# Seeding four RNN steps at once, and transposing before the tanh

## The chip, the cores and the metric

The kernel runs on one core of a Trainium2 chip. The metric is the time of one execution on the device in microseconds. The engines are named as in the profile: PE is the matrix engine (TensorE), PEld its weight loads, DVE is VectorE, ACT is ScalarE, POOL is GpSimd, SP is the engine that issues most DMAs.

## The reference, cut to what matters

The kernel computes two layers, each an attention branch and a feed-forward branch, on x of 8 sequences (batch B), 512 steps and 256 features in float32. The change lies in the last branch: a plain recurrent network over the 512 steps, followed by a mixture of 16 experts with two chosen per token.

```python
xW = jnp.einsum('ntd,dh->nth', x, Wx) + b

def step(h_prev, xw_t):
    h_next = jnp.tanh(xw_t + h_prev @ Wh)
    return (h_next, h_next)
_, hs = jax.lax.scan(step, h0, jnp.swapaxes(xW, 0, 1))
...
return x + _mlp(x, shared_wg, shared_wu, shared_wd) + expert_weighted
```

In the second part of the quotation x stands for the states hs. Each step needs the state of the step before, so the 512 steps run one after another: 8 rows of 256 features times a matrix of 256 x 256, plus the input's share xW, then tanh.

## The kernel before, in words

Earlier stages (attention of layer 0, an LSTM of 512 steps, routed heads, attention of layer 1) are not touched. The last stage is `rnn_moe`; it begins at 3272 us of the span.

**The recurrence.** The state is kept transposed, with the 256 features as 2 x 128 partitions, in `ring`: 16 steps (a chunk, `XB`) x 2 halves k x 32 columns, of which the first 8 hold the batch. `rnn_step` does one step t. Its 8 recurrent matmuls (L1375) take the state of the step before as the stationary operand (128 rows x 8 columns, for each half k) and 64 columns of `Wh` as the moving operand, for j = 0..3. Matmul j writes 8 rows at partitions 32j of the accumulator `pg` (128 x 64, one of two that alternate); so the four j lie in four column groups of PE. A float32 matmul is two passes on PE, so 8 matmuls are 16 PE records, in four passes of the four groups. The input's share of a step, `xw`, is brought into `pg` before that by four "seed" matmuls (L1359): the stationary operand is 8 columns of the identity matrix that pick the 8 rows of step t out of a chunk of 128 rows (b, t). The seeds of step t+1 are issued right behind the recurrent matmuls of step t. Then ACT takes the tanh of the whole `pg` (128 x 64) into `h` (L1379), and DVE transposes `h` in blocks of 32 x 32 into the ring's slot (L1380).

**What else shares the loop.** Each step ends with `consume()`, which issues the DVE and ACT work left over from the step before (`M.later`), and `advance(...)`, which issues one piece of PE work: the projection of a later chunk's input (`rnn_project`, L1349), a piece of a finished chunk (`Experts.chunk`: router L1428, turning the states L1439, shared expert L1450 to L1455, its second matmul L1468, residual L1472), or a piece of an expert tile (`Experts.tiles`: gate matmuls L1597, transposes of the next tile L1587, down matmul L1613). The order on PE, ACT and DVE is exactly the order of these calls (`manual_schedule`); each engine works through its list in order. So on PE a step is: recurrent matmuls, seeds, the piece of other work; on ACT: tanh, then later work; on DVE: transpose, then later work. A chunk's pieces fall on steps t%16 = 2, 3, 4, 7 and 8; tiles and projections take the others, where there are any. A tile takes three steps: a first gate step (half of the gate matmuls, first transpose), a second gate step (the other half, second transpose) and a down step. The transposes of a tile share a PSUM tile and are copied out one by one:

```python
nc.tensor.transpose(pt[:, k, :], X[m][:, k * P : (k + 1) * P], K.ident)
later(lambda: nc.scalar.copy(xT[:, k, :], pt[:, k, :]))
```

These are L1587 and L1588. The gate's later work is a sigmoid on ACT (L1606) and a product on DVE (L1607). The LSTM stage (L677 to L696, 457 to 1710 us) has the same layout of its state, but transposes the sums on DVE first and lets ACT work on the transposed block.

**Waits.** An instruction waits for its semaphores; where it has more than one, the others are waited for by an instruction of the sequencer ahead of it (EVENT_SEMAPHORE in the profile), in the order in which the program lists them.

**POOL.** It copies a finished chunk of the ring into `hT` (L1421), gathers x for projections and residuals (L1336), and issues the scatters and gathers of rows (L1558, L1650); some of these are held back until `M.pace`, which is the transpose of the current step.

Of the kernel before, what the change touches and what calls it, by code (L numbers as in the profile page):

```python
# [9 lines left out]
F32 = mybir.dt.float32  # L10
I32 = mybir.dt.int32
U32 = mybir.dt.uint32
AF = mybir.ActivationFunctionType
# [5 lines left out]
P = 128  # L19
B = 8  # L20
S = 512
# [1306 lines left out]
XB = 16  # L1328
# [3 lines left out]
def chunk_x(K, M, n, tag):  # L1332

    xc = M.hp.tile([P, 2, P], F32, name=tag, tag=tag)
    for k in range(2):
        K.nc.gpsimd.tensor_copy(xc[:, k].rearrange("p (b t) -> p b t", b=B), K.xT[:, k, :, n * XB : (n + 1) * XB])  # L1336
    return xc
# [14 lines left out]
            yield 1  # L1352


def rnn_seed(K, M, t):

    pick = K.ident.rearrange("p (b t) -> p t b", b=B)
    for j in range(4):
        K.nc.tensor.matmul(  # L1359
            M.pg[t % 2][32 * j : 32 * j + B], pick[:, t % XB, :], M.xw[:, t // XB, 64 * j : 64 * j + 64], start=True, stop=False  # L1360
        )


def rnn_step(K, M, t):


    nc, mm = K.nc, K.nc.tensor.matmul
    at = t % XB
    if at == 0:
        M.last, M.ring = M.ring, M.rg.tile([P, XB, 2, 32], F32, name="ring", tag="ring")  # L1370
    pg = M.pg[t % 2]
    for k in range(2):
        hp = K.h0T[:, k, :] if t == 0 else (M.ring[:, at - 1, k, 0:B] if at else M.last[:, XB - 1, k, 0:B])
        for j in range(4):
            mm(pg[32 * j : 32 * j + B], hp, M.wh[:, k, 64 * j : 64 * j + 64], start=False, stop=(k == 1))  # L1375
    if t + 1 < S:
        rnn_seed(K, M, t + 1)
    h = M.hp.tile([P, 64], F32, name="h", tag="h")
    nc.scalar.activation(h, pg, AF.Tanh)  # L1379
    M.pace = nc.vector.transpose(M.ring[:, at].rearrange("p k b -> p (k b)"), h)  # L1380


class Experts:
# [30 lines left out]
    def chunk(self, c, ring):  # L1414

        K, M, NE = self.K, self.M, self.NE
        nc, mm, later = K.nc, K.nc.tensor.matmul, M.later
        t0 = (self.first + c) * XB
        hT = M.hp.tile([P, 2, B, XB], F32, name="hT", tag="hT")
        for k in range(2):  # L1420
            nc.gpsimd.tensor_copy(hT[:, k], ring[:, :, k, 0:B].rearrange("p t b -> p b t"))  # L1421
        xc = chunk_x(K, M, t0 // XB, "xc")
        hk = [hT[:, k].rearrange("p b t -> p (b t)") for k in range(2)]
        yield 0
        yield 0
        pr = M.pd.tile([P, NE], F32, name="pr", tag="pd")
        for k in range(2):
            mm(pr, hk[k], M.wr[:, k, :], start=(k == 0), stop=(k == 1))  # L1428
        rl = M.sp.tile([P, NE], F32, name="rl", tag="rl")

        def logits():
            nc.vector.tensor_tensor(rl, pr, M.rb, ALU.add)
            nc.scalar.activation(rl, rl, AF.Sigmoid)

        later(logits)
        yield 1
        pt = M.pd.tile([P, 2, P], F32, name="pt", tag="pd")
        for k in range(2):
            nc.tensor.transpose(pt[:, k, :], hk[k], K.ident)  # L1439
        hr = M.ap.tile([P, D], F32, name="hr", tag="hr", bufs=16)  # L1440
        self.hr.append(hr)

        def turned():
            nc.scalar.copy(hr, pt.rearrange("p k t -> p (k t)"))
            nc.vector.max(out=self.top[:, c, :], in_=rl)
            nc.vector.max_index(out=self.topi[:, c, :], in_max=self.top[:, c, :], in_values=rl)

        later(turned)
        pw = [M.pgu.tile([P, P], F32, name="pw", tag="gu")]
        mm(pw[0], M.wg[:, 0, :], hk[0], start=True, stop=False)  # L1450
        yield 1
        mm(pw[0], M.wg[:, 1, :], hk[1], start=False, stop=True)
        pw.append(M.pgu.tile([P, P], F32, name="pw", tag="gu"))
        for k in range(2):
            mm(pw[1], M.wu[:, k, :], hk[k], start=(k == 0), stop=(k == 1))  # L1455
        a = M.sp.tile([P, P], F32, name="a", tag="a")

        def act():
            nc.scalar.activation(a, pw[0], AF.Sigmoid)
            nc.vector.tensor_tensor(a, pw[0], a, ALU.mult)  # L1460
            nc.vector.tensor_tensor(a, pw[1], a, ALU.mult)

        later(act)
        yield 1
        yield 0
        yield 0
        pd = M.pd.tile([P, D], F32, name="pd", tag="pd")
        mm(pd, a, M.wd, start=True, stop=False)  # L1468
        yield 1
        pj = pd.rearrange("p (j k r) -> p k j r", j=4, k=2)  # L1470
        for k in range(2):
            mm(pj[:, k], xc[:, k], K.ident, start=False, stop=(k == 1))  # L1472
        acc = M.ap.tile([P, D], F32, name="acc", tag="acc", bufs=27)
        self.acc.append(acc)
        later(
            lambda: nc.vector.tensor_tensor(
                acc.rearrange("p (j k r) -> p j k r", j=4, k=2),
                pd.rearrange("p (j k r) -> p j k r", j=4, k=2),
                hr.rearrange("p (k j r) -> p j k r", j=4, k=2),
                ALU.add,  # L1480
            )
        )
        yield 1
# [182 lines left out]
def rnn_moe(K, out):  # L1666


    nc, inp = K.nc, K.inp
    with ExitStack() as es:  # L1670
        wp = K.pool(es, "m_w")
        M = Scope()
# [34 lines left out]
        M.sp = K.pool(es, "m_s", 4)  # L1707
        M.wp = K.pool(es, "m_e", 7)
        M.ap = K.pool(es, "m_a", 2)
        M.rg = K.pool(es, "m_rg", 3)  # L1710
        M.hp = K.pool(es, "m_h", 2)
        M.psx = K.pool(es, "m_px", 1, PSUM)
        psg = K.pool(es, "m_pg", 1, PSUM)
        M.pg = [psg.tile([P, 64], F32, name=f"pg{i}") for i in range(2)]
        for t in M.pg:
            nc.vector.memset(t, 0.0)
        M.pxt = K.pool(es, "m_xt", 1, PSUM)
        M.pgu = K.pool(es, "m_gu", 2, PSUM)
        M.pd = K.pool(es, "m_pd", 2, PSUM)
        M.ring = None  # L1720
        xc = chunk_x(K, M, 0, "xp")
        px = M.psx.tile([P, D], F32, name="px", tag="px")
        for k in range(2):
# [1 line left out]
        nc.vector.tensor_tensor(M.xw[:, 0, :], px, M.rbias, ALU.add)  # L1725
        due = []
        M.later = due.append
        rnn_seed(K, M, 0)
        E = mybir.EngineType

        def consume():
# [32 lines left out]
        nb, at = -1, 0  # L1764
        with K.tc.manual_schedule(engines={E.PE, E.Activation, E.DVE}):
            for t in range(S):
                if t % XB == 0:
                    if t == XB * sum(BLOCKS[: nb + 1]):
                        nb += 1
                        block, at = Experts(K, M, nb), 0  # L1770
# [187 lines left out]
```

## Time and profile before

| | |
|---|---|
| median of 14 runs | 4100.07 us (4095.39 to 4108.0) |
| the profiled execution, its own time | 4097.13 us |
| its span | 4095.3 us |
| mean granted PE clock | 0.968 |
| busy share PE / PEld / DVE / ACT / POOL | 87% / 56% / 58% / 36% / 15% |
| the loop of 512 steps | 3286 to 3908 us, preceded by 8 us in which step 0 waits for ACT |
| granted PE clock in the loop | 0.94 |
| after the loop | 187 us for the last tiles and the output |

A line of the groups gives line, engine, operation, what is written and read, the shapes and the count; then the busy time in us and the mean ns of one; then how long the engine was idle before them and what ended most of that. In the order in time each line has start and duration in us, engine, line, operation and count, and in brackets the idle time before it and its releaser. Kernel lines in the profile of before are those of the listing above.

### The profile page before, as it was taken

The page shows a single profiled execution, that of the slowest core. Times are in us where ns is not written, and L with a number is a line of the kernel's source. Part 1 is how long each engine was busy: PE and PEld are TensorE (multiplying, and loading weights), DVE is VectorE, ACT ScalarE, POOL GpSimd, SP SyncE. Part 2 cuts the span into 40 slices and gives each one's busy share as a digit, 9 for nine tenths or more (in the row PEclk, how much of TensorE's full clock was granted, in tenths as well). Part 3 has the DMA queues.
Part 4 walks back from the last instruction along what each step waited for, and adds up shares of the span by engine and source line. Part 5 has one row for each costly group of instructions (what it writes and reads, how often), then busy time and mean ns, then how long its engine had stood idle before and what let it go on. Part 6 is the DMA issues. An engine that isn't in the chain of part 4 may idle for free.

```text
span 4095.3 us, 150218 instructions
## 1 busy us (share of the span) xinstructions
PE 3551.9 (87%) x64484; PEld 2275.7 (56%) x64484; DVE 2395.6 (58%) x8916; ACT 1463.1 (36%) x5391; POOL 606.2 (15%) x1250
## 2 busy tenths in 40 slices
PE   8899888888888888699988998999899887999885
PEld 5533455555555555456645555555555555767564
DVE  4488666666666666466657667656766533333332
ACT  3111233333333333245534435444444322333242
POOL 1010000000000000111012222222212221030412
PEclk9899999999999999899989999999999998999897
DMA  3122000000000000200000000000000022443476
GB/s 105 42 67 73 18 20 15 21 15 20 5 4 4 4 4 4 76 24 24 1 2 2 1 1 1 1 1 1 1 1 1 13 96 68 118 149 105 129 245 204
DMA packets 104844, 173.11 MB, mean 42 GB/s; under 512 B 12576, under 2 KB 71872, under 8 KB 103792
## 3 DMA queue, kind: packets, MB, share of 16 engines
q1 hardware_dynamic: 79792, 114.23, 9.1%
q0 software_dynamic: 12064, 34.34, 2.6%
q10 hardware_dynamic: 12320, 14.94, 1.1%
q8 instruction: 505, 8.27, 0.9%
q14 instruction: 163, 1.34, 0.1%
HBM read 124.53 MB, written 40.10 MB: 40 GB/s over the span
## 4 chain that ended last, share of the span: by engine, by line
PE 42%; DVE 8%; ACT 3%; DMA 2%; issue 2%; ACTq 0%; SPq 0%; POOL 0%; DVEq 0%; POOLq 0%
PE pg L1375 5%; PE pe L1202 4%; PE pp L1166 4%; DVE sm L1218 3%; PE pt L1241 3%; PE pg L1597 3%; PE px L1276 3%; PE po L1257 3%; DMA x<-xs 2%; PE pe L893 2%; PE pp L869 1%; PE pv L1186 1%; PE py L1613 1%; PE pt L913 1%; PE pg L1359 1%
## 5 line engine op out<-in xcount | busy, mean ns | idle before, releaser
L677 PE MATMUL pgi<-wh,ring 128*8 128x128 f32 x8176 | 319.3, 273 | 214.9 <-DVE ring L696 212.2
L1222 ACT ACTIVATE sm<-sm,nm 128x388 f32<-128x388 f32 (+3 forms) x512 | 282.9, 553 | 346.9 <-DVE nm L1218 346.8
L684 ACT ACTIVATE X<-G 128x32 f32<-128x32 f32 x512 | 117.1, 229 | 679.9 <-DVE G L683 679.9
L1380 DVE STREAM_TRANSPOSE ring<-h 128x64 f32<-128x64 f32 x512 | 125.6, 245 | 396.4 <-ACT h L1379 382.1
L677 PEld LDWEIGHTS pgi<-wh,ring 128*8 128x8 f32 x8176 | 177.1, 89 | 279.2 <-DVE ring L696 277.7
L1241 PE MATMUL pt<-ident,sm 128*128 128x128 f32 x1280 | 214.7, 284 | 104.6 <-ACT eT L1243 55.4
L683 DVE STREAM_TRANSPOSE G<-pgi 128x128 f32<-128x128 f32 x512 | 161.8, 316 | 244.8 <-PE pgi L677 244.8
L1379 ACT ACTIVATE h<-pg 128x64 f32<-128x64 f32 x512 | 114.7, 224 | 456.4 <-PE pg L1375 419.6
L1241 PEld LDWEIGHTS pt<-ident,sm 128*128 128x128 f32 x1280 | 144.2, 142 | 224.4 <-DVE eT L1243 86.9
L1375 PE MATMUL pg<-wh,ring 128*8 128x64 f32 x8176 | 219.9, 228 | 55.3 <-DVE ring L1380 51.0
L1166 PE MATMUL pp<-hn,wqkv 128*128 128x512 f32 x512 | 244.4, 604 | 5.0 <-DVE hn L1151 5.0
L1232 POOL COPY pme<-sm 128x4 f32<-128x4 f32 x512 | 119.6, 234 | 818.9 <-DVE sm L1231 814.6
L1375 PEld LDWEIGHTS pg<-wh,ring 128*8 128x8 f32 x8176 | 122.0, 91 | 163.7 <-DVE ring L1380 132.3
L677 PE MATMUL pgg<-wh,ring 128*8 128x64 f32 x8176 | 208.6, 219 | 1.3 <-issue 1.3
L677 PE MATMUL pgo<-wh,ring 128*8 128x64 f32 x8176 | 208.8, 219 | 0.1
L657 PE MATMUL pgi<-xw,ident 128*8 128x128 f32 x4096 | 207.7, 273 | 0.5 <-DVE xw L647 0.5
L1218 DVE CUSTOM_DVE_ANT_0 sm<-pe,mask 128x260 f32<-128x260 f32 (+2 forms) x384 | 141.7, 425 | 107.6 <-PE pe L1202 103.8
L696 DVE SCALAR_TENSOR_TENSOR ring<-to,th 128x16 f32<-128x16 f32 x512 | 89.6, 175 | 174.7 <-ACT th L695 174.7
L1243 ACT COPY eT<-pt 128x128 f32<-128x128 f32 (+3 forms) x256 | 108.4, 423 | 212.8 <-PE pt L1241 212.7
L1231 DVE TENSOR_SCALAR sm<-sm,rc 128x388 f32<-128x388 f32 (+3 forms) x512 | 177.3, 389 | 9.1
L1597 PE MATMUL pg<-xT,w 128*128 128x128 f32 x992 | 172.5, 300 | 10.6 <-DVE a L1460 8.9
L1202 PE MATMUL pe<-kt,qt 32*128 32x132 f32 (+3 forms) x2048 | 177.8, 461 | 0.0
(503 smaller groups left out, 7887.8 us busy)
## 6 DMA issues: line engine op xcount, KB each, us to landing
w<-in_experts_dram SPq DMA_DIRECT2D x124, 384.0 KB
cb<-order POOLq DMA_DIRECT2D x32, 512.0 KB, 4.1
x<-xs SPq DMA_DIRECT2D x124, 128.0 KB
ys<-y SPq DMA_DIRECT2D x124, 128.0 KB
xs<-zero ACTq DMA_DIRECT2D x2, 4736.0 KB
w<-in_ada_w_dram SPq DMA_DIRECT2D x16, 512.0 KB
w<-in_moh_w_dram SPq DMA_DIRECT2D x32, 192.0 KB
out_dram<-acc SPq DMA_DIRECT2D x32, 128.0 KB
```

What stands on the lines that cost most here:

```text
L657: mm(dst[32 * j : 32 * j + B], pick[:, t % XB, :], xw[:, j * 256 + lo : j * 256 + hi], start=True, stop=False)
L677: mm(dst[32 * j : 32 * j + B], hp, wh[:, k, j * 256 + lo : j * 256 + hi], start=False, stop=(k == 1))
L683: nc.vector.transpose(G[:, 0:2].rearrange("p g k b -> p (g k b)"), pgi[t % 2].rearrange("p g n -> p (g n)"))
L1166: mm(pp, T.wqkv[:, k, 0 : 2048].rearrange("p (i g h n) -> p i g h n", i=2, g=4, h=2)[:, i, g, h], self.hn[b][:, k, :], start=(k == 0), sto ...
L1202: mm(pe[a][:, 0 : w - lo], q[r, h, at], k[r, h, lo:w], start=(h == 0), stop=(h == 1))
L1218: nc.vector.tensor_tensor_reduce(out=sm[a][:, lo:w], in0=pe[a][:, 0 : w - lo], in1=T.mask[:, S - n + lo : 4 + S], scale=-1.0 / 8.0, scalar ...
L1222: nc.scalar.activation(sm[a][:, 0:w], sm[a][:, 0:w], AF.Exp, bias=nm[:, a : a + 1], scale=-1.0, accum_out=su[:, a : a + 1])
L1231: nc.vector.tensor_scalar(sm[a][:, 0:w], sm[a][:, 0:w], rc[:, a : a + 1], None, ALU.mult)
L1241: nc.tensor.transpose(pt[:, j, :], sm[a][:, 4 + j * P : 4 + (j + 1) * P], K.ident)
L1375: mm(pg[32 * j : 32 * j + B], hp, M.wh[:, k, 64 * j : 64 * j + 64], start=False, stop=(k == 1))
L1380: M.pace = nc.vector.transpose(M.ring[:, at].rearrange("p k b -> p (k b)"), h)
L1597: mm(pg, W[m][:, k * D + g * P : k * D + (g + 1) * P], X[m][:, k, :], start=(k == 0), stop=(k == 1))
```

## The change

The accumulator now holds four steps at once. Each of the four column groups has 32 rows instead of 8: four steps of 8 rows. A seed matmul has 32 stationary columns, which pick 32 rows (four steps) of `xw`; one such matmul for one j is issued per step, so that the four j of the next block of four steps are seeded during the present one. Blocks begin at t = 1, 5, 9, 13, ...; the block that begins at t%16 = 13 takes three steps from one chunk and one from the next, which takes two seed matmuls per j (`ends`), issued in steps t%16 = 9 to 12.

The recurrent matmuls have the ring's whole 32 columns as the stationary operand. Only the 8 columns that belong to the step (`w = 8 * (t % 4)`) hold a state; the others are zero, from a memset at the start, and add nothing to the rows of the other steps. The three rings are fixed tiles now.

The order of the last two operations is turned round: DVE transposes the whole accumulator out of PSUM into `g` (128 x 64), and ACT takes the tanh of the step's 16 columns (2 halves x 8) out of `g` into the ring. PE then waits for ACT and not for DVE. Copying a chunk to `hT` becomes four POOL copies, one per t%4, in place of two.

```diff
-def rnn_seed(K, M, t):
-    pick = K.ident.rearrange("p (b t) -> p t b", b=B)
-    for j in range(4):
-        K.nc.tensor.matmul(
-            M.pg[t % 2][32 * j : 32 * j + B], pick[:, t % XB, :], M.xw[:, t // XB, 64 * j : 64 * j + 64], start=True, stop=False
-        )
+class Picks:
+    def __init__(self, K, pool):
+        nc = K.nc
+        self.mm = nc.tensor.matmul
+        self.steps = pool.tile([P, 16, B], F32, name="steps")
+        nc.vector.tensor_copy(self.steps, K.ident.rearrange("p (b t) -> p t b", b=B))
+        self.ends = pool.tile([P, 2, 32], F32, name="ends")
+        nc.vector.memset(self.ends, 0.0)
+        nc.vector.tensor_copy(self.ends[:, 0, 0:24].rearrange("p (t b) -> p t b", b=B), self.steps[:, 13:16, :])
+        nc.vector.tensor_copy(self.ends[:, 1, 24:32], self.steps[:, 0, :])
+    def seed(self, dst, t, xw, nxt):
+        at = t % 16
+        if at == 0:
+            self.mm(dst, self.ends[:, 1], nxt, start=True, stop=False, skip_group_check=True)
+        elif at == 13:
+            self.mm(dst, self.ends[:, 0], xw, start=True, stop=False, skip_group_check=True)
+            if nxt is not None:
+                self.mm(dst, self.ends[:, 1], nxt, start=False, stop=False, skip_group_check=True)
+        else:
+            self.mm(dst, self.steps[:, at : at + 4, :].rearrange("p t b -> p (t b)"), xw, start=True, stop=False, skip_group_check=True)
+def rnn_seed(K, M, t, j):
+    n = t // XB
+    at = slice(64 * j, 64 * j + 64)
+    M.pick.seed(
+        M.pg[(t + 3) // 4 % 2][32 * j : 32 * j + 32], t, M.xw[:, n, at],
+        M.xw[:, 0 if t == 0 else n + 1, at] if n + 1 < S // XB else None,
+    )
...
-    if at == 0:
-        M.last, M.ring = M.ring, M.rg.tile([P, XB, 2, 32], F32, name="ring", tag="ring")
-    pg = M.pg[t % 2]
+    M.ring, last = M.rings[t // XB % 3], M.rings[(t // XB - 1) % 3]
+    pg = M.pg[(t + 3) // 4 % 2]
     for k in range(2):
-        hp = K.h0T[:, k, :] if t == 0 else (M.ring[:, at - 1, k, 0:B] if at else M.last[:, XB - 1, k, 0:B])
+        hp = M.h0[:, k] if t == 0 else (M.ring[:, at - 1, k] if at else last[:, XB - 1, k])
         for j in range(4):
-            mm(pg[32 * j : 32 * j + B], hp, M.wh[:, k, 64 * j : 64 * j + 64], start=False, stop=(k == 1))
-    if t + 1 < S:
-        rnn_seed(K, M, t + 1)
-    h = M.hp.tile([P, 64], F32, name="h", tag="h")
-    nc.scalar.activation(h, pg, AF.Tanh)
-    M.pace = nc.vector.transpose(M.ring[:, at].rearrange("p k b -> p (k b)"), h)
+            mm(pg[32 * j : 32 * j + 32], hp, M.wh[:, k, 64 * j : 64 * j + 64], start=False, stop=(k == 1), skip_group_check=True)
+    if 0 < t <= S - 4:
+        rnn_seed(K, M, (t + 3) // 4 * 4 + 1, (t + 3) % 4)
+    g = M.hp.tile([P, 2, 32], F32, name="g", tag="g")
+    M.pace = nc.vector.transpose(g.rearrange("p k b -> p (k b)"), pg)
+    z, w = 8 * ((t + 3) % 4), 8 * (t % 4)
+    nc.scalar.activation(M.ring[:, at, :, w : w + 8], g[:, :, z : z + 8], AF.Tanh)
...
-        for k in range(2):
-            nc.gpsimd.tensor_copy(hT[:, k], ring[:, :, k, 0:B].rearrange("p t b -> p b t"))
+        for i in range(4):
+            nc.gpsimd.tensor_copy(hT[:, :, :, i:XB:4], ring[:, i:XB:4, :, 8 * i : 8 * i + 8].rearrange("p q k b -> p k b q"))
...
-        M.rg = K.pool(es, "m_rg", 3)
+        M.rings = [wp.tile([P, XB, 2, 32], F32, name=f"ring{i}") for i in range(3)]
+        M.h0 = wp.tile([P, 2, 32], F32, name="h0")
+        for t in (*M.rings, M.h0):
+            nc.gpsimd.memset(t, 0.0)
+        nc.vector.tensor_copy(M.h0[:, :, 24:32], K.h0T)
+        M.pick = Picks(K, wp)
...
-        rnn_seed(K, M, 0)
+        for t in range(2):
+            for j in range(4):
+                rnn_seed(K, M, t, j)
```

More of the change, by code (lines that the diff above doesn't have):

```diff
@@ L1714, in rnn_moe @@
         M.pg = [psg.tile([P, 64], F32, name=f"pg{i}") for i in range(2)]
-        for t in M.pg:
-            nc.vector.memset(t, 0.0)
         M.pxt = K.pool(es, "m_xt", 1, PSUM)
@@ L1719, in rnn_moe @@
         M.pd = K.pool(es, "m_pd", 2, PSUM)
-        M.ring = None
         xc = chunk_x(K, M, 0, "xp")
```

## The prediction

> **What bounds the kernel now.** I read the busy shares, then the instruction groups of the RNN loop, then its order in time. TensorE (PE) is busy 87% of the span, but in the loop (3286 to 3908 us, 512 steps, 1.22 us each) that is no bound by itself: its matmuls wait for the state.
>
> ```profile
> L1380 DVE STREAM_TRANSPOSE ring<-h 128x64 f32<-128x64 f32 x512 | 125.6, 245 | 396.4 <-ACT h L1379 382.1
> L1379 ACT ACTIVATE h<-pg 128x64 f32<-128x64 f32 x512 | 114.7, 224 | 456.4 <-PE pg L1375 419.6
> L1375 PE MATMUL pg<-wh,ring 128*8 128x64 f32 x8176 | 219.9, 228 | 55.3 <-DVE ring L1380 51.0
> L1375 PEld LDWEIGHTS pg<-wh,ring 128*8 128x8 f32 x8176 | 122.0, 91 | 163.7 <-DVE ring L1380 132.3
> ```
>
> Each of the three waits for the one before: a ring. A step with no other work on PE has a median of 1036 ns, and the records add up to it: 191 from the first recurrent matmul to the start of the last, 219 that one, 67 until ACT starts, 224 tanh, 33 until DVE, 245 transpose, 55 until PE starts again (1034).
>
> Other work shares the steps, always queued on PE behind the recurrent matmuls and seeds, on ACT behind the tanh, on DVE behind the transpose. The second gate step of an expert tile shows what that does, in order of time:
>
> ```profile
> 3686.28 0.41 PE L1375 MATMUL pg<-wh,ring 128*8 128x64 f32 x16
> 3686.50 0.29 PE L1359 MATMUL pg<-xw,ident 128*8 128x64 f32 x8
> 3686.73 0.71 PE L1597 MATMUL pg<-xT,w 128*128 128x128 f32 x4
> 3686.75 0.22 ACT L1379 ACTIVATE h<-pg 128x64 f32<-128x64 f32 x1 [0.98 <-PE pg L1375]
> 3686.88 0.27 ACT L1606 ACTIVATE ea<-pg 128x128 f32<-128x128 f32 x1
> 3687.01 0.24 DVE L1380 STREAM_TRANSPOSE ring<-h 128x64 f32<-128x64 f32 x1 [0.65 <-ACT h L1379]
> 3687.03 0.27 ACT L1588 COPY xT<-pt 128x128 f32<-128x128 f32 x1
> 3687.36 0.33 PE L1587 MATMUL pt<-ident,x 128*128 128x128 f32 x1
> 3687.62 0.17 PEld L1375 LDWEIGHTS pg<-wh,ring 128*8 128x8 f32 x12
> ```
>
> The ring is ready at 3687.26, but PE starts the next step only at 3687.62: in front of it stands transpose L1587, which waits for ACT's copy L1588, which is queued behind tanh and sigmoid. 191+219+67+121 (tanh to sigmoid, start to start)+158 (to the copy)+272+54+259 (transpose to next step) = 1341; the records have 1340. So ACT's queue bounds this kind, PE's work the first gate step, the ring the empty one. Counting all 512 steps by the PE work in them:
>
> - empty 90, at 1036; router (L1428) 31 and turn (L1439) 31, at 1036 and 1044: the ring
> - projection (L1349) 62, down (L1613) 66, L1468 31, at 1081, and L1472 31, at 1094: PE, 45 to 58 above the ring
> - first gate step 64 at 1202, shared expert (L1452, L1455) 31 at 1317: PE
> - second gate step 51 at 1340, 14 gate steps after the shared expert at 1660 to 2060: ACT or DVE results that PE waits for.
>
> **The change part by part.**
>
> *Order of the two engines.* The ring becomes PE, DVE, ACT, PE. Nearest rows are the LSTM's, which already goes that way:
>
> ```profile
> L687 DVE STREAM_TRANSPOSE G<-pgo x512: 249/250/252, 457.9 to 1708.9; 128x64 f32<-128x64 f32 x171
> L688 ACT ACTIVATE X<-G x512: 197/199/218, 458.0 to 1709.0; 128x16 f32<-128x16 f32 x171
> L695 ACT ACTIVATE th<-X x512: 215/215/218, 458.7 to 1709.7; 128x16 f32<-128x16 f32 x171
> ```
>
> The columns are least/median/most ns. A transpose of 64 columns out of PSUM takes 250 (+5). Tanh of 16 columns takes 215 after a wait (L695), 199 right behind another; I take 215 (-9). So the tanh's four times smaller width buys almost nothing. PE to DVE is 68 in the LSTM (L677 to L683), DVE to ACT 33, ACT to PE 52 to 55 (L1588 to L1587): no change.
> [...]
>
> *A second wait.* In the changed program's order, 288 of 512 transposes wait first for PE and then for ACT (the tanh two steps back, which reads the same g buffer), and 154 tanhs for DVE first and then for POOL (ring slots) or ACT. What the first of two waits costs when it is the late one is in the trace: tanhs L1379 that list PE first start 127 after PE, the others 67; L1380 with POOL in second place starts 104 after ACT, else 33; L684 93 against 32. I take +60 each; ends 0 and 70.
>
> *Stationary columns.* The 8 recurrent matmuls now load 32 columns. Weight loads last 90 ns at 8 columns, 138 at 64 (L255), 190 at 128: 0.83 per column, so 20 more for 32. Within a step passes follow each other every 56 to 59 ns and the next load runs under the present pass; only the first load is bare: L255's second pass starts 107 after its first, L1375's 59, and its further passes every 58, L1375's 56. Interpolated: +22 per step. Ends: 0 and +53 (L255's whole 64 columns).
>
> *Seeds.* Three of four seed matmuls go. But the four stood in different column groups and ran together: 2 passes, 112 ns after the last recurrent pass. One matmul alone still has 2 passes of 56: PE gains only the spread between the groups, 0 to 20 (I take 10). In 4 of every 16 steps (t%16 = 9 to 12) two seeds fall on the same group: 4 passes, so 112 more, 102 net.
>
> *What queues behind the waiting tanh.* ACT's later work now waits for transpose and tanh: its start moves from 67 after PE to 67+250+33 = 350, or 410 with the second wait. DVE's later work moves forward by about the same, but depends on ACT's sigmoid, so gains nothing. The second gate step becomes 191+22+219+127+250+33+121+158+272+54+259 = 1706.
>
> *Beside the path.* hT takes four POOL copies of 64 elements instead of two of 128 (411 each): between 234 (L1232, 4 elements) and 411 each, 0.1 to 0.8 us more per chunk; PE reads hT a median 2.0 us after it is written, four times under 0.7, so nothing, at most 2 us in all. Three POOL memsets of 1024 elements (0.4 us at 388 columns, L1002: about 1 us each) delay the first projection by 1 to 3 us, but ACT is issuing DMA L1680 until 3285.9, and the first tanh cannot start before; if that cover were gone, 3 us. Step 0 then ends without the transpose, -0.3. SP issues nothing new. Paced scatters on POOL follow the transpose as before.
>
> **Sum.**
> - Ring: 191+22+219+67+250+33+215+55 = 1052; plus 60 in 56% and 60 in 30% of steps: mean 1104, +68. Empty: 90 x 68 = 6.1 us. Router and turn, at t%16 = 2 and 3 where every tanh lists POOL: 62 x 110 = 6.8.
> - The 190 steps at 1081 to 1094: PE +12, overtaken by the ring in over half, mean +22 = 4.2; 43 of them have two seeds: +102 = 4.4.
> - First gate steps: 64 x 12 = 0.8, 29 of them with two seeds, +112: 3.2. Shared expert: 0.7.
> - Second gate steps: 51 x 366 = 18.7. The 14 others: ACT's shift of 283 = 4.0.
>
> Together +48.9 us. The profiled execution took 4097.1 (span 4095.3), 3 under the median of the runs; the median goes from 4100.1 to **4149**. With every term at its low end (no second-wait cost, loads hidden) the sum is about 25; with the load at 53, 64.
>
> **Rivals.**
> 1. *The clock is relieved: not slower.* PE's granted clock is 0.94 over the loop, 0.5 in stretches of 7 to 14 us where steps are empty; there empty steps take 1240, router 1725, turn 1807, shared expert 2340. If four times the columns keep the clock up, the loop gets back at most its excess over the kinds' medians, 621-591 = 30 us (591: the count of each kind above times its median). It decides only if the rest is under 30, that is near my low end: 25-30, 4095. Against it: the same number of passes runs, fewer of the seeds'.
> 2. *The clock gets worse.* Steps are longer and PE rests more in them. If half of the 31 chunks (now 5 to 8) fell in half clock: 9 x (0.69+0.76+1.02) + 20 x 0.2 = 26 more, 4175.
> 3. *Weight loads of the four groups run one after another.* 4 x 27 = 107 per pass instead of 56: 204 per step in place of 22, 4242. Against it: L255's two loads of 64 columns begin 6 ns apart and last no longer for it. [...]
> 4. *Second waits and loads cost nothing:* 4125.
>
> **How the numbers follow.** My forecast 68%, rival 1 12%, rival 2 10%, rival 3 4%, rival 4 6%. The range 4112 to 4190 holds the forecast (alone: 4128 to 4170), rivals 2 and 4 and little of 1. A difference under 0.2% (8 us) cannot be told from none: rival 1 gives 8% faster and 4% same; all else is slower.
>
> **What would show it.** Transposes near 250 that start 67 or 127 after PE; tanh 199 to 215; weight loads near 110; empty steps 1050 to 1170; L1597 followed by a longer wait of L1587 for ACT; second gate steps near 1700; the end of the span unchanged after the loop. Wrong if tanh falls well under 199, if second gate steps stay near 1340, or if the loop's clock rises above 0.94 by much.

## The result, and the profile after

The changed kernel takes **4154.42 us** (median of 6 runs, 4152.18 to 4160.29) against 4100.66 for the kernel before (28 runs): a ratio of 1.0133, with a 95% interval of 1.0123 to 1.0143. That is 53.8 us slower, where 4149 (48.9 slower) was forecast.

The profiled execution of the changed kernel took 4158.2 us, 3.8 above its median, and that of before lay 3 to 4 below its own; so the two traces differ by 61.1 us of span, some 7 more than the medians do. The trace splits these 61.1:

| stretch | before, us | after, us | difference |
|---|---|---|---|
| until the second step's first matmul | 3286.6 | 3286.8 | +0.3 |
| from there to the first matmul of the last step | 620.9 | 677.9 | +57.0 |
| from there to the end | 187.8 | 191.7 | +3.9 |

The last line is not a trace of the change: over all the kernels below this tail lies anywhere between 183 and 195 us, whatever was edited. The loop holds the result. In the profile of after, the seeds stand on L1373 to L1379, the recurrent matmuls on L1402, the transpose on L1406, the tanh on L1408, the copy into `hT` on L1449, the tiles' transposes and copies on L1615 and L1616, the gate matmuls on L1625, sigmoid and product on L1634 and L1635.

The instruction groups of the loop after, which answer to the four lines shown of before:

```profile
L1406 DVE STREAM_TRANSPOSE g<-pg 128x64 f32<-128x64 f32 x512 | 127.7, 249 | 401.6 <-PE pg L1402 390.9
L1408 ACT ACTIVATE ring<-g 128x16 f32<-128x16 f32 x512 | 110.4, 216 | 532.7 <-DVE g L1406 467.6
L1402 PE MATMUL pg<-wh,ring 128*32 128x64 f32 x8176 | 235.0, 237 | 60.2 <-ACT ring L1408 57.5
L1402 PEld LDWEIGHTS pg<-wh,ring 128*32 128x32 f32 x8176 | 147.3, 115 | 172.6 <-ACT ring L1408 143.9
```

Nothing here has become cheap. The transpose takes 249 ns out of PSUM (245 out of SBUF before), the tanh 216 ns on a quarter of the columns (224 before). The mean weight load went from 91 to 115 ns. The ring's releasers have changed places as planned: DVE waits for PE, ACT for DVE, PE for ACT. So the same ring runs with nearly the same three durations, and most of what is dearer must lie between the instructions.

The second gate step, in order of time (seeds, most weight loads and the product on DVE are left out). This is the same step of the loop as the one shown of before:

```profile
3718.35 0.43 PE L1402 MATMUL pg<-wh,ring 128*32 128x64 f32 x16
3718.92 0.25 DVE L1406 STREAM_TRANSPOSE g<-pg 128x64 f32<-128x64 f32 x1 [0.76 <-PE pg L1402]
3718.92 0.71 PE L1625 MATMUL pg<-xT,w 128*128 128x128 f32 x4
3719.20 0.21 ACT L1408 ACTIVATE ring<-g 128x16 f32<-128x16 f32 x1 [1.10 <-DVE g L1406]
3719.32 0.26 ACT L1634 ACTIVATE ea<-pg 128x128 f32<-128x128 f32 x1
3719.48 0.26 ACT L1616 COPY xT<-pt 128x128 f32<-128x128 f32 x1
3719.79 0.33 PE L1615 MATMUL pt<-ident,x 128*128 128x128 f32 x1 [0.16 <-ACT xT L1616]
3720.05 0.43 PE L1402 MATMUL pg<-wh,ring 128*32 128x64 f32 x16
```

The new state is ready at 3719.41 (3719.20 + 0.21). PE starts the next step at 3720.05, 0.6 us later, because transpose L1615 stands in front of it and waits for the copy L1616. That copy stands on ACT behind tanh and sigmoid, as before; but the tanh now starts 0.85 us after PE's first recurrent matmul and not 0.47. The step takes 1.70 us; before it took 1.34. The last matmul of the 16 ends at 3718.78, and the transpose starts 0.14 later, not 0.07.

That last gap can be seen for all steps in the views of the two lines (counts, then least/median/most ns):

```profile
L1406 DVE STREAM_TRANSPOSE g<-pg x512: 237/250/251, 3279.7 to 3965.2; 128x64 f32<-128x64 f32 x171
L1406 DVEq EVENT_SEMAPHORE  x357: 21/21/21, 3289.5 to 3963.3; - x179
```

```profile
L1408 ACT ACTIVATE ring<-g x512: 199/216/218, 3286.6 to 3965.5; 128x16 f32<-128x16 f32 x171
L1408 ACTq EVENT_SEMAPHORE  x154: 17/17/38, 3286.5 to 3949.5; - x154
```

The same lines of before, where the tanh follows PE and the transpose follows the tanh:

```profile
L1379 ACTq EVENT_SEMAPHORE  x512: 17/17/17, 3286.0 to 3906.9; - x171
L1380 DVEq EVENT_SEMAPHORE  x29: 21/21/21, 3343.3 to 3890.0; - x29
```

An EVENT_SEMAPHORE in these records is an instruction of the engine's sequencer that waits for one of two semaphores ahead of the work. In the kernel after, DVE has 357 of them; in 269 steps the transpose starts about 138 ns after PE's last matmul, in 194 steps 67. ACT has 154; in 150 steps the tanh starts 93 ns after the transpose, in 356 steps 33. Their number alone does not decide: before, every tanh has one, and 435 of the 512 start 67 ns after PE all the same. What decides is which semaphore it waits for, and the records name it. After, it is PE's, the late one, for 288 transposes, and none of these starts at 67 ns; it is ACT's, long done, for 69, and 67 of these start at 67 ns.

Matched step by step, and sorted by the PE work in them as in the prediction, the medians and the sums over the loop are:

| PE work in the step | count | median ns, before and after | sum us, before and after | change | forecast |
|---|---|---|---|---|---|
| none (empty) | 90 | 1036, 1218 | 99.5, 111.9 | +12.4 | +6.1 |
| router, turn | 62 | 1036 and 1044, 1182 | 75.9, 81.0 | +5.1 | +6.8 |
| projection, down, L1468, L1472 of before (without step 0) | 189 | 1081 to 1094, 1095 to 1182 | 210.9, 222.7 | +11.8 | +8.6 |
| first gate step | 64 | 1203, 1224 | 77.0, 81.2 | +4.2 | +4.0 |
| shared expert | 31 | 1317, 1338 | 48.8, 49.3 | +0.5 | +0.7 |
| second gate step | 51 | 1341, 1703 | 68.4, 87.5 | +19.1 | +18.7 |
| late gate steps (most of them right after the shared expert) | 14 | 2059, 2293 | 27.6, 31.6 | +4.0 | +4.0 |

Only one line is far off, the empty steps; the projections add to it. The larger part of that is not the clock: the 47 empty steps that ran at full clock in both traces grew by 114 ns on average, where 68 were forecast. Of the 288 transposes that wait for PE first, 70 fall on empty steps, so that 78% of the 90 have one; the forecast had taken the average over all steps, 56%. In 13 of the 47 the transpose starts still later, 218 ns or more after PE; in the five of these at t%16 = 6, DVE is still at the work left over from the shared expert, and the other eight stay unexplained. The rest is the clock. Over the loop the granted PE clock was 0.94 before; here are three windows of after and one of before (window, its length, busy us and instructions of PE, PEld, DVE, ACT and POOL, granted clock, DMA share, GB/s):

```profile
3287.00:3965.00 678.00, 597.95 (x11004) 434.43 (x11000) 234.73 (x1015) 177.36 (x872) 146.07 (x323) 0.92 0.32 97
3400.00:3417.00 17.00, 14.66 (x219) 11.25 (x219) 3.71 (x17) 2.69 (x13) 0.71 (x3) 0.50 0.01 2
3840.00:3965.00 125.00, 102.25 (x1886) 76.03 (x1881) 40.80 (x168) 28.65 (x142) 47.17 (x71) 0.80 0.38 118
```

```profile
3286.00:3908.00 622.00, 561.19 (x13821) 398.10 (x13822) 227.16 (x1016) 185.59 (x874) 131.44 (x258) 0.94 0.35 107
```

In both traces the granted clock is either full or half, 1.0 or 0.5, and nothing between: 3400 to 3417 is one whole stretch at 0.50. In the loop the stretches at half clock last 79 us before and 110 us after. In the stretch shown, PE counts as busy 86% of the time, with no gap above 0.6 us; the share is that high partly because a recurrent matmul's record lasts 314 ns there and 219 at full clock.

So I sorted the 511 steps by the clock they ran at in both traces. 427 ran at full clock in both, and grew from 504.2 to 547.4 us: **+43.2**. 43 ran at half clock in both (for at least half of the step): +3.1. Of the others, 29 lost clock in whole or part (+11.7) and 11 gained some (-2.0); one is mixed in both (+0.7). These 41 grew by 10.4 us together; the growth of their kinds at full clock makes up 3.6 of that. The change itself, at an unchanged clock, is therefore worth some 50 us in this pair of traces, and the clock some 7.

### The profile page after: what moved, and what is told of

It reads as the page before. It is cut to its first block, busy times and chain, and to the rows that moved or that the text cites. A ratio compares the mean times of both kernels' runs of the same rounds, so it can differ in the third digit from the quotient of the medians.

```text
span 4156.4 us, 144659 instructions
## 1 busy us (share of the span) xinstructions
PE 3587.8 (86%) x61668; PEld 2314.3 (56%) x61668; DVE 2405.5 (58%) x8919; ACT 1454.9 (35%) x5391; POOL 623.5 (15%) x1318
## 3 DMA queue, kind: packets, MB, share of 16 engines
q14 instruction: 164, 1.34, 0.1%
## 4 chain that ended last, share of the span: by engine, by line
PE 41%; DVE 9%; ACT 4%; DMA 2%; issue 2%; ACTq 0%; SPq 0%; DVEq 0%; POOL 0%; POOLq 0%
PE pg L1402 5%; PE pp L1166 4%; PE pe L1202 4%; DVE sm L1218 3%; PE pt L1241 3%; PE px L1276 3%; PE po L1257 3%; PE pg L1625 2%; DMA x<-xs 2%; PE pe L893 2%; PE pp L869 1%; PE pv L1186 1%; PE py L1641 1%; PE pt L913 1%; DVE g L1406 1%
## 5 line engine op out<-in xcount | busy, mean ns | idle before, releaser
L1406 DVE STREAM_TRANSPOSE g<-pg 128x64 f32<-128x64 f32 x512 | 127.7, 249 | 401.6 <-PE pg L1402 390.9
L1408 ACT ACTIVATE ring<-g 128x16 f32<-128x16 f32 x512 | 110.4, 216 | 532.7 <-DVE g L1406 467.6
L1402 PE MATMUL pg<-wh,ring 128*32 128x64 f32 x8176 | 235.0, 237 | 60.2 <-ACT ring L1408 57.5
L1402 PEld LDWEIGHTS pg<-wh,ring 128*32 128x32 f32 x8176 | 147.3, 115 | 172.6 <-ACT ring L1408 143.9
L1625 PE MATMUL pg<-xT,w 128*128 128x128 f32 x992 | 173.1, 301 | 14.1 <-DVE a L1488 11.5
```

The costliest lines, as they stand in the source:

```text
L1402: mm(pg[32 * j : 32 * j + 32], hp, M.wh[:, k, 64 * j : 64 * j + 64], start=False, stop=(k == 1), skip_group_check=True)
L1406: M.pace = nc.vector.transpose(g.rearrange("p k b -> p (k b)"), pg)
L1625: mm(pg, W[m][:, k * D + g * P : k * D + (g + 1) * P], X[m][:, k, :], start=(k == 0), stop=(k == 1))
```

## The experiments

The theory at the outset: the time goes (1) into waits with two semaphores, where the late one comes first, (2) into later work on ACT, which now stands behind transpose and tanh, (3) into some 20 ns of wider weight loads per step. Rivals: the wide columns themselves are dear, or four steps in one accumulator are; or a transpose out of the bank that PE has just written is slow to start, whatever it waits for; or all of it is clock.

The kernels ran on three chips, and each is compared with the kernel before on its own chip. The first four below ran beside 4099.13 us for the kernel before, the next four beside 4146.02 on another chip, the last four beside 4101.19 on a third.

**The order alone.** The kernel before, with only the two operations turned round, on the step's 8 columns:

```diff
-    h = M.hp.tile([P, 64], F32, name="h", tag="h")
-    nc.scalar.activation(h, pg, AF.Tanh)
-    M.pace = nc.vector.transpose(M.ring[:, at].rearrange("p k b -> p (k b)"), h)
+    g = M.hp.tile([P, 2, 32], F32, name="g", tag="g")
+    M.pace = nc.vector.transpose(g.rearrange("p k b -> p (k b)"), pg)
+    nc.scalar.activation(M.ring[:, at, :, 0:B], g[:, :, 0:B], AF.Tanh)
```

> The kernel before with only the order of its last two operations turned round: transpose of the sums out of PSUM into g, then tanh of 16 columns into the ring; 8 stationary columns and four seeds per step as before. Theory (ACT's later work queues behind a tanh that now waits for the transpose, and a second wait costs 60 ns when the first is the late one): second gate steps go from 1341 to about 1685 (1703 less the 22 of the wide load), empty steps to about 1030 or 1090, loop +30 us, about 4131. Rival PE (the loss is on PE: wide loads and doubled seeds): the order costs nothing, 4096 to 4106. Rival clock (the loss is more time at half clock): within 10 us of before.

Measured: 4128.85 us, 1.0069 [1.0053, 1.0086], so +29.7. Second gate steps have a median of 1679 ns, empty ones at full clock 1100. More than half of the slowdown is the order alone, without one column or seed changed.

**The columns alone.** The changed kernel with the order of before: tanh of the whole bank, then a transpose of all four steps' columns into the slot. The slot's other 24 columns are then no longer zero, so the kernel does not compute the reference; its instructions on PE are those of the changed kernel.

```diff
-    g = M.hp.tile([P, 2, 32], F32, name="g", tag="g")
-    M.pace = nc.vector.transpose(g.rearrange("p k b -> p (k b)"), pg)
-    z, w = 8 * ((t + 3) % 4), 8 * (t % 4)
-    nc.scalar.activation(M.ring[:, at, :, w : w + 8], g[:, :, z : z + 8], AF.Tanh)
+    h = M.hp.tile([P, 64], F32, name="h", tag="h")
+    nc.scalar.activation(h, pg, AF.Tanh)
+    M.pace = nc.vector.transpose(M.ring[:, at].rearrange("p k b -> p (k b)"), h)
```

> The changed kernel with the old order of the last two operations: tanh of the whole accumulator, then transpose into all 32 columns of the ring slot. 32 stationary columns and one seed matmul per step stay. The zero columns are no longer zero and the states stand in wrong columns, so the output is not the reference's; the instructions on PE are those of the changed kernel. Theory: what is left is the wide load (22 ns x 512 = 11 us where it is on the path) and the double seeds in steps 9 to 12 of 16 (about 8 us): +15 to +21 us, about 4118; second gate steps near 1365. Rival PE: nearly the whole loss, 4145 to 4155. Rival clock: if wide columns raised or lowered the clock, the granted clock in the loop would differ from 0.94 with the same steps otherwise.

Measured: 4112.34 us, 1.0038 [1.0026, 1.005], so +13.2, a little under what was expected. The time from the first recurrent matmul to the start of the last is 212 ns (191 before), and the second gate steps are back at 1360. Order and columns add up to 42.9 of the 53.8; in the traces, where the loop grows by 35.2 and 15.7 us, to 50.9 of 57.0. The rest stays open. It is hardly the waits that rings as fixed tiles bring, whose slots are taken over from POOL's copies (154 extra waits in the tanh of the changed kernel, 30 with the order alone): the columns alone already pay for such waits, on DVE.

```profile
L1407 DVEq EVENT_SEMAPHORE  x116: 21/21/21, 3341.9 to 3908.3; - x116
```

Before, these are 29. In 115 steps of this kernel the transpose starts about 103 ns after the tanh, in most others 32; 86 such steps more than before, at 70 ns, are up to 6 of its 13 us.

**Later work first.** The changed kernel with the later work of DVE and ACT issued between the transpose and the tanh:

```diff
     M.pace = nc.vector.transpose(g.rearrange("p k b -> p (k b)"), pg)
     z, w = 8 * ((t + 3) % 4), 8 * (t % 4)
+    consume()
     nc.scalar.activation(M.ring[:, at, :, w : w + 8], g[:, :, z : z + 8], AF.Tanh)
...
-                rnn_step(K, M, t)
-                consume()
+                rnn_step(K, M, t, consume)
```

> The changed kernel with the work left over from the step before issued ahead of the tanh on ACT (it stays behind the transpose on DVE). ACT is then idle no more while PE and DVE work, and the copy that the second transpose of a tile waits for no longer stands behind the tanh. Theory: second gate steps fall from 1703 to the first gate steps' 1224 or close to it, the 14 late gate steps by some 300; loop -30 us against the changed kernel, about 4124. Rival PE: no more than 5 us, since PE's instructions and their order are unchanged. Rival clock: unchanged, or a gain spread over all kinds of steps.

Measured: 4119.64 us, 1.0049 [1.0032, 1.0065], some 34 us under the changed kernel's 1.0133. The second gate steps fell from 1703 to 1217 ns, the late ones from 2293 to 1800, while the turn steps rose from 1183 to 1286. So the place in ACT's queue was the largest single price of the change. It was a price that the kernel before paid too, in part.

**Blocks of four that begin at 0.** The changed kernel with blocks at t = 0, 4, 8, ..., so that no block spans two chunks and no step has two seeds per j (shortened):

```diff
-        if at == 0:
...
-        elif at == 13:
...
-        else:
+        if True:
             self.mm(dst, self.steps[:, at : at + 4, :].rearrange("p t b -> p (t b)"), xw, start=True, stop=False, skip_group_check=True)
...
-    if 0 < t <= S - 4:
-        rnn_seed(K, M, (t + 3) // 4 * 4 + 1, (t + 3) % 4)
+    if t < S - 4:
+        rnn_seed(K, M, t // 4 * 4 + 4, t % 4)
```

> The changed kernel with the blocks of four steps beginning at t = 0, 4, 8, ..., so that none straddles two chunks and no step has two seed matmuls in one column group. Theory: first gate steps, projection and down steps at t%16 = 9 to 12 lose their extra 112 ns: about 70 steps, -7 to -8 us against the changed kernel, about 4147; all else as in the changed kernel. Rival (the second seed of the same group runs beside the first, or is hidden): no difference.

Measured: 4145.65 us, 1.0115 [1.0098, 1.0132]. The median is 9 us under the changed kernel's and the intervals overlap; the first gate steps went from 81.2 to 79.1 us in sum, and the 189 PE-bound ones (projections, down steps, L1468 and L1472 of before) from 222.7 to 215.3. By these steps the double seeds cost about what was forecast; the times alone do not show it, and they are a small part.

**32 columns in the kernel before.** The kernel before with the ring's whole 32 columns as the stationary operand of recurrent matmuls and seeds (the rest are zeros), four seeds per step and the old order:

```diff
-            M.pg[t % 2][32 * j : 32 * j + B], pick[:, t % XB, :], M.xw[:, t // XB, 64 * j : 64 * j + 64], start=True, stop=False
+            M.pg[t % 2][32 * j : 32 * j + 32], M.pick[:, t % XB, :], M.xw[:, t // XB, 64 * j : 64 * j + 64], start=True, stop=False
...
-        hp = K.h0T[:, k, :] if t == 0 else (M.ring[:, at - 1, k, 0:B] if at else M.last[:, XB - 1, k, 0:B])
+        hp = M.h0[:, k] if t == 0 else (M.ring[:, at - 1, k] if at else M.last[:, XB - 1, k])
...
-            mm(pg[32 * j : 32 * j + B], hp, M.wh[:, k, 64 * j : 64 * j + 64], start=False, stop=(k == 1))
+            mm(pg[32 * j : 32 * j + 32], hp, M.wh[:, k, 64 * j : 64 * j + 64], start=False, stop=(k == 1))
```

> The kernel before with 32 stationary columns in every recurrent matmul and seed: 8 of the state and 24 zeros. Four seeds per step, one step per accumulator, tanh before transpose, all as before. Theory: the bare first load of a step is 24 columns longer, 0.83 ns each: first to second pass 81 instead of 59 ns, issue of a step's recurrent matmuls 191 to 213; +22 ns on nearly every step, loop +11 us, about 4110. Rival (the four groups share one load path): passes at about 107 instead of 56 ns, +100 us. Rival (loads hidden): no difference. Read with the run that has the old order and 32 columns (+13 us): what is above this run there is the double seeds.

Measured: 4161.71 us, 1.0032 [1.002, 1.0044], +13 by the ratio on a chip on which the kernel before took 4146. The issue (from the first recurrent matmul to the start of the last) is 212 ns, the empty step at full clock 1055, that is 20 over the 1035 of before. Between this kernel (+13) and the columns alone with seeds of four steps (+13.2, other chip) these runs show no gain from seeding four steps at once. In the trace of before a load lasts 90 ns at 8 columns (L1375) and 190 at 128 (L1186), 0.83 ns per column; estimated by that, 24 more columns cost 20 ns. Here the median load went from 90 to 110 and the issue from 191 to 212, in agreement with that difference.

**16 buffers of g in the changed kernel.** No transpose then waits for a tanh two steps back:

```diff
-    g = M.hp.tile([P, 2, 32], F32, name="g", tag="g")
+    g = M.hp.tile([P, 2, 32], F32, name="g", tag="g", bufs=16)
```

> The changed kernel with 16 buffers for g instead of 2: the transposes' second wait, for the tanh that last read the buffer, falls away in 284 of 288 steps; in return some 80 more tanhs list DVE first and then ACT. Theory (a second wait costs 60 ns where the first is the late one): transposes start 67 ns after PE in nearly all steps, tanhs 93 after DVE in more than before; net about -7 us against the changed kernel, about 4147. Rival (the second wait is free): no difference, within 2 us of 4154.

Measured: 4185.84 us, 1.0099 [1.0083, 1.0115], against 1.0133 of the changed kernel on other chips. Transposes start 67 ns after PE in 415 steps (194 before this edit), second gate steps take 1632 in place of 1703. The size of the gain could not be told across chips, so the edit was repeated with its pair on one chip, below.

**Later work first in the kernel before.** Nothing else is changed:

```diff
     h = M.hp.tile([P, 64], F32, name="h", tag="h")
+    consume()
     nc.scalar.activation(h, pg, AF.Tanh)
...
-                rnn_step(K, M, t)
-                consume()
+                rnn_step(K, M, t, consume)
```

> The kernel before, with one line moved: the work left over from the step before is issued ahead of the tanh on ACT (and ahead of the transpose on DVE). Theory: the copy that the second transpose waits for no longer stands behind the tanh; second gate steps fall from 1341 to about 1203, the late gate steps after the shared expert too, while tanhs are held up by at most some 100 ns where sigmoid and copy run late; loop -17 us, about 4083. Rival (the path goes through tanh wherever ACT has other work, so putting work in front of it costs what it saves): 4095 to 4110.

Measured: 4127.06 us beside 4146.02, 0.9954 [0.994, 0.9967]: faster than the kernel before, by 0.46%.

**Order, later work first and 16 buffers together**, with 8 columns (the edits of the order alone, of later work first and of 16 buffers):

> The kernel before (8 columns, four seeds) with three edits: transpose before tanh, the left-over work ahead of the tanh on ACT, 16 buffers for g. Theory: the new order has no cost of its own once ACT's queue and the second waits are out of the way: ring 191+219+67+250+33+215+55 = 1030, second gate steps near 1203; loop -8 to -9 us against before, about 4091. Rival (the order itself is slower on this chip): above 4100.

Measured: 4137.99 us, 0.998 [0.9971, 0.9989], the 8 us less that were expected. Second gate steps take 1203 ns. With its two prices removed, the turned order is still some 11 us behind the old order with the same later work: turn steps take 1195 in place of 1094, late gate steps 1709 in place of 1203, where ACT's later work, now ahead of the tanh, can still wait for DVE's, which stands behind the transpose. That last reading is argued from the order of the queues, and no run isolates it.

**The second wait by itself.** First the order alone once more, and beside it the same with 16 buffers of g, which is a difference of one argument:

> The kernel before with only the order turned round (transpose of 64 columns first, then tanh of 16 columns, 8 stationary columns), a second time, beside the next run. It gave 1.0069 on the first chip, with empty steps of 1100 ns at full clock, second gate steps of 1679 ns and 265 transposes that start about 140 ns after PE. Both theories expect the same: 1.005 to 1.0085.

> The same with 16 buffers of g in place of 2, so that no transpose waits for the tanh two steps back. Theory (the late first of two waits costs 60 to 70 ns): the transposes start 67 ns after PE in over 400 steps; empty, router and turn steps at full clock go from 1100 to 1030 ns, second gate steps from 1679 to about 1610, projections from 1100 to 1081: 95 x 0.07 + 51 x 0.07 + 60 x 0.02 = 11 us under the run beside it, ratio near 1.004. Rival (the 140 ns belong to a transpose out of the bank that PE has just written, whatever it waits for): 0 us, 1.007.

Measured: 4132.47 us, 1.0071 [1.0055, 1.0088], and 4121.85 us, 1.0048 [1.0032, 1.0063]: 10.6 us less, where 11 was expected. The two intervals overlap a little; the steps do not. (The profile with 16 buffers also has 7 us less at half clock, so a few of the 10.6 may be clock.) Empty steps at full clock go from 1100 to 1031 ns, router steps from 1099 to 1030, second gate steps from 1680 to 1610. The view of the transposes, first with two buffers, then with 16:

```profile
L1379 DVE STREAM_TRANSPOSE g<-pg x512: 239/250/251, 3276.3 to 3941.3; 128x64 f32<-128x64 f32 x171
L1379 DVEq EVENT_SEMAPHORE  x359: 21/21/21, 3275.0 to 3939.3; - x180
```

```profile
L1379 DVE STREAM_TRANSPOSE g<-pg x512: 238/250/251, 3279.3 to 3932.3; 128x64 f32<-128x64 f32 x171
L1379 DVEq EVENT_SEMAPHORE  x7: 21/21/21, 3277.9 to 3312.4; - x7
```

And, with 16 buffers, the view of the tanh, for a comparison further on:

```profile
L1380 ACTq EVENT_SEMAPHORE  x30: 17/17/38, 3286.3 to 3913.6; - x30
```

The transpose is the same 250 ns out of the same bank; what went away are 352 of the sequencer's waits, and with them the 70 ns. The rival (a fresh bank is slow to start) is out. An empty step without them is 1031 ns, 4 under the step of before, so in a step with no other work the turned ring as such costs nothing.

**All of it removed, with 32 columns and four steps seeded at once.** The changed kernel with blocks from 0, 16 buffers and later work first (the three edits shown above):

> The change with blocks of four steps that begin at t = 0, 4, 8, ... (no step has two seeds), 16 buffers of g, and the later work of DVE and ACT issued ahead of the tanh. Theory (the change's price is the second wait, the late sigmoid and copy, and 20 ns of wider loads): empty steps 1035 - 5 + 22 = 1052 ns at full clock, second gate steps about 1220, the 190 PE-bound steps 1100 to 1110: 64 x 0.017 + 190 x 0.022 + 64 x 0.02 + 2 - 51 x 0.12 - 14 x 0.34 = -2 us, and up to 8 more in half clock: 0.9995 to 1.002. Rival (32 columns or the seeds of four steps cost more than their loads show): 20 us or more, 1.005 and above.

Measured: 4104.39 us, 1.0011 [1.0, 1.0022], inside what the theory gave and far from the rival's 1.005. Of the 53.8 us about 50 are gone, and no column and no seed of four steps was taken out. The second gate steps take 1216 ns. The empty steps take 1109 at full clock and not the 1052 that I expected, and the tanh's waits show why:

```profile
L1403 ACT ACTIVATE ring<-g x512: 198/216/218, 3284.8 to 3913.4; 128x16 f32<-128x16 f32 x171
L1403 ACTq EVENT_SEMAPHORE  x199: 17/17/38, 3284.7 to 3898.0; - x199
```

199 tanhs still have an extra wait (30 above, with rings from a pool), and 193 start 93 ns after the transpose. I had counted the second wait as removed, and had removed it on DVE only. Rings from a pool would be the next thing to try there; that was not tried.

**The faster version again**, on a chip on which the kernel before takes 4101:

> The kernel before with nothing changed but that DVE's and ACT's later work is issued ahead of the step's tanh and transpose; it gave 0.9954 on another chip. Theory (the second gate steps wait for the copy that stands behind tanh and sigmoid): second gate steps 1203 ns in place of 1341, the late gate steps 1203 in place of 2059: 51 x 0.14 + 14 x 0.75 = 17 to 18 us less, 0.9955. Rival (the gain there was that chip's clock): within 0.2% of the kernel before.

Measured: 4085.05 us, 0.9958 [0.9946, 0.9971], 16 us faster than before. The second gate step of this kernel (its lines from L1379 on have numbers one higher than in the kernel before):

```profile
3678.38 0.28 ACT L1607 ACTIVATE ea<-pg 128x128 f32<-128x128 f32 x1 [0.50 <-PE pg L1598]
3678.38 0.41 PE L1375 MATMUL pg<-wh,ring 128*8 128x64 f32 x16
3678.55 0.26 ACT L1589 COPY xT<-pt 128x128 f32<-128x128 f32 x1
3678.84 0.71 PE L1598 MATMUL pg<-xT,w 128*128 128x128 f32 x4
3678.86 0.22 ACT L1380 ACTIVATE h<-pg 128x64 f32<-128x64 f32 x1
3679.12 0.24 DVE L1381 STREAM_TRANSPOSE ring<-h 128x64 f32<-128x64 f32 x1
3679.38 0.27 PE L1588 MATMUL pt<-ident,x 128*128 128x128 f32 x1
3679.59 0.41 PE L1375 MATMUL pg<-wh,ring 128*8 128x64 f32 x16
```

Sigmoid and copy run while PE is still at the recurrent matmuls, the tanh follows at 3678.86, 0.48 after PE's start as ever, and L1588 follows the gate matmuls without a wait. The step is 1.21 us and PE's work sets it. The price is small: turn steps go from 1044 to 1094.

## Why the prediction was right, point by point

- **The order of the two engines** (+5 and -9): 250 and 216 ns, as the LSTM's rows gave them. The kernel with 16 buffers shows the turned ring at 1031 against 1035.
- **A second wait** (+60, ends 0 and 70; 288 transposes and 154 tanhs): shown. It is 70 on DVE (269 steps start at about 138) and 60 on ACT (150 steps). The pair with 2 and 16 buffers prices DVE's part at 10.6 us in the kernel with 8 columns.
- **Stationary columns** (+22): 21 in the median issue, 191 to 212, in the changed kernel, in the columns alone and in the kernel before with 32 columns.
- **Seeds** (10 saved, +102 in double steps): the first gate steps gave +4.2 for +4.0, and the blocks from 0 returned 7 us by the ratios and 9 by the medians, against an expected 7.
- **What queues behind the waiting tanh** (+366 for the second gate step, 1706): 1703 measured. Taking it away returned 34 us. That is the 18.7 + 4.0 of the forecast and what this queue had cost the kernel before: 51 times 0.12 (1341 to 1217) and 14 times 0.26 (2059 to 1800), together some 32.
- **Beside the path** (nothing for the copies into `hT` and the memsets): the copies take a median 305 ns, inside the 234 to 411, and the loop starts 0.3 us later in the trace. Both covers held.
- **The sum.** At an unchanged clock the trace gives some +50 for the forecast +48.9. The second gate steps, all at full clock, gave 19.0 (forecast 18.7). Router and turn were a little oversized: 110 ns each forecast, a mean of 100 at full clock, since only 33 of the 62 had both late waits.
- **The terms that were mis-sized** are two. One is the second wait in the empty steps: the forecast spread it evenly, as 60 in 56% of the steps, and got 68 ns for each empty one; at full clock they grew by 114, because the late first wait falls on 70 of the 90 and costs 70, and because in some the transpose waits for more. That is 10 of their 12.4 us, against 6.1. The other is the clock, which the sum held constant: half clock in the loop went from 79 to 110 us, worth some 7 us in the trace. It is the first rival's opposite and the second rival's direction, at less than its price (26). That 53.8 came so near 48.9 is partly luck: these 4 and 7 us stood against some 2 too many in the router, turn and PE-bound steps, and the two traces differ by 7 us more than the medians do.
- **The rivals.** Not relieved: the mean clock in the loop fell from 0.94 to 0.92. Loads of four groups are not serial: 212 ns of issue and not 395. Second waits and loads are not free.

What stays open is why the clock got worse. Leaving out the slower chip, the seven profiles of kernels that transpose first, the changed one among them, spent 103 to 120 us of the loop at half clock, the three of kernels that take the tanh first 72 to 79, the one with the columns alone (75) among them. So there the order goes with it, and the wide columns do not. On the slower chip that is not so: there the most, 175 us, belongs to a kernel that takes the tanh first (the kernel before with 32 columns), against 144 and 148 for the two that transpose first and 131 for the kernel before with later work first. A guess would be that the order works through the idle time that PE gets within a step; no run shows that idle time lowers the clock, and the kernel with 16 buffers has empty steps of 1031 ns, shorter than those of before, and still spent 103 us at half clock. One profile of each kernel does not settle it.

## What to carry to other kernels

Before turning two dependent operations round, ask what is queued behind the one that will now wait longer; here a copy that PE needs stood there, and taking it out of the way returned 34 us, more than everything the change touched on PE (some 13). When an operation gets a new buffer, count its buffers: a wait for an older reader that has long been done still cost some 60 to 70 ns in the ring here, where it made the late wait the first of two. And where an engine has work from the step before that is already ready, issue it ahead of the operation that waits for the present step; in this kernel that edit alone was worth 0.4%, while the change it was meant to explain cost 1.3%.

## What the runs showed of the hardware that was not expected

- A wait that is satisfied was not free in these traces. In that of after, with two semaphores and the late one in the sequencer's separate instruction, 269 DVE transposes start about 138 ns after PE in place of 67, and 150 ACT tanhs 93 ns after DVE in place of 33. With the late one in the instruction itself, the separate wait cost nothing: 67 ns again, in 67 of 69 transposes.
- A chip can be 1.1% slower at one and the same kernel: 4146.02 against 4099.13 and 4101.19 for the kernel before. The version with later work first spent 131 us of the loop at half clock there, and 72 on another chip.
- The half-clock stretches in the loop are multiples of 3.4 us (3.4, 6.8, 10.2, 13.7, 17.1 and 20.5 us in the trace of after). Of the 74 steps after with some half clock 38 are empty and 23 more are router, turn and shared expert steps, and in the stretch at 3400 us PE has short gaps only, none above 0.6 us. No run here shows what sets them off.
